# Attention scores of all four sequences behind the second gate product, and other places for turns, routing and picking in the last group

## Chip, cores and metric

The kernel runs on one core of one Trainium2 chip. The metric is device time in microseconds (us), the median of several runs; lower is better. All data is float32.

## What is computed

The input is 64 audio signals of 80000 samples. Each is cut into 157 frames of 512 samples (the last one padded), and each frame gets a discrete cosine transform, which gives a matrix of 157 tokens x 512 channels per signal. One transformer layer follows:

```
h = frames @ D^T                                     # DCT, 157 x 512 per signal
x = layernorm(h)
k, q = tanh(x Wk) pi, tanh(x Wq) pi                  # 4 sets x 8 planes of phases
total = sum over sets, planes of  w_s * Re( cumsum(e^{ik} V) e^{-iq} ),  V = x Wv + bv
pos   = the same with fixed phases of the position
gate  = sigmoid(x Wg + bg)
h = h + x + (gate * total + (1 - gate) * sigmoid(pw) * pos) / sqrt(8 t) @ Wo + bo
x2 = layernorm(h)
idx = argmax(mean over tokens of x2 @ Wg' + bg')     # one of 16 experts per signal
h = h + softmax value of idx * (x2 We[idx] + be[idx])
```

Because the phases are few, the cumulative sums are written as a causal attention: scores are cosines of phase differences, summed over sets and planes, times a mask.

## The kernel before, in words

The 64 signals are worked on in 16 groups of four (`GB = 4`, `NG = 16`). Of the 157 tokens of a signal the first 128 make one full tile; the 29 left over of all four signals, the tails, share a fifth tile (index `GB`). The order of all instructions on every engine is written out by hand, so what stands earlier in the code stands earlier in each engine's queue. For a group g from 1 to 15 one turn of the main loop is:

1. `project_and_values(g)`: phases of group g, the values V, and routing and picking for group g-1. `pick` ends with the row numbers of the chosen experts, `fetch` (L707) starts four gathering DMAs of 1 MB of expert weights each from the POOL queue.
2. `gate(g)` (L871): five small gathering DMAs for the expert biases (`bias`, L744) and two additions of the value bias (`add_bv`, L348, 128x1024 each) go into the POOL queue, together with the subtraction of one frame (`fold_once`, L97). Then the gate is computed by a Strassen-like scheme with seven products in the order 1, 2, 6, 5, 7, 3, 4. `gate_product` (L534) issues eight matmuls into one PSUM tile; `gather` (L288) then adds the tile to the partial sums on VectorE (L286; product 1 is copied by ScalarE, L295). The products share three PSUM tiles in rotation (`ps_mm`, 3 buffers). Product 5 is kept in its tile (`held`) until the second of the two additions that follow product 7; product 4 gets that same tile.
3. Between the products stand the scores: `scores(0)` and `scores(2)` each make two matmuls (L559), one VectorE multiplication of the PSUM result by a mask (L561) and one VectorE addition of two SBUF operands (`att` and `share`, L562, 128x314). `scores_of_tails` makes one matmul (L566), one multiplication (L567) and one addition of two SBUF operands (L570, 128x116). Their PSUM tiles come from the other pool (`ps_tr`, 2 buffers). Before the change `scores(0)` stands behind the first product, `scores(2)` behind the third, `scores_of_tails` behind the fourth.
4. `experts_and_embedding(g)`: the expert products of group g-1 mixed with the transform of group g+1.
5. `attention(g)`: reading values with the scores, and the output product.

Group 0 has a start of its own. After the loop stands the code of the last group (L962 to L998): the expert products of group 14 (`expert(g - 1, ...)`), between which group 15 is normalised (`normal2`, ScalarE, L650), transposed (`turn_x2`: four transposes on TensorE, L166, and a copy out of PSUM), routed (`route`, `route_sum`, `route_spread`) and picked; then four weight fetches, `pick_gate`, five bias gathers, the two expert products of group 14 that are left, and the five of group 15 in the order 0, 1, 2, tails, 3. `expert` calls `between(c)` ahead of the two matmuls of each quarter c of its contraction. The first two fetches go to the rooms of `wv` and `wg`, which are free by then; the other two to the weight buffers that group 14's first two experts leave. The bias `be_last` gets the router's weight and the residual added (`add_bias`, L755) before the expert's PSUM tile is added (L774), and only then is that PSUM tile free.

`place` (L169) writes the copy of a transposed tile. For a full tile it uses the engine that is passed as `copy`; for the tails' tile it used ScalarE always.

Of the kernel before, what the change touches and what calls it, by code (L numbers as in the profile page):

```python
# [22 lines left out]
P = 128  # L23
C = D // P
H = D // 2
GB = 4
# [13 lines left out]
ORDER = [GB, *range(GB)]  # L40
# [3 lines left out]
def audio_tower(ctx: ExitStack, tc: tile.TileContext, a, out):  # L44
# [15 lines left out]
    nc = tc.nc  # L60
# [14 lines left out]
    def psum():  # L75

        return ps_mm.tile([P, 2, 512], F32, tag="mm", name="mm")

    def bank():
        return ps_tr.tile([P, 512], F32, tag="tr", name="tr")  # L80
# [10 lines left out]
    def fold_once(g, m):  # L91

        if g < NG:
            ft = S[g]["frame", m]
            even = p2.tile([P, 2, P], F32, tag="even", name="even")
            nc.vector.tensor_tensor(even, ft[:, :2, :], ft[:, 2:, :], ALU.add)
            nc.gpsimd.tensor_tensor(ft[:, :2, :], ft[:, :2, :], ft[:, 2:, :], ALU.subtract)  # L97
            S[g]["even", m] = even

    def fold_twice(g, m):  # L100

        if g < NG:
            ft, even = S[g]["frame", m], S[g].pop(("even", m))
            nc.vector.tensor_tensor(ft[:, 2, :], even[:, 0, :], even[:, 1, :], ALU.add)
            nc.vector.tensor_tensor(ft[:, 3, :], even[:, 0, :], even[:, 1, :], ALU.subtract)
# [57 lines left out]
    def transposed(x):  # L163
        tr = bank()
        for c in range(C):
            nc.tensor.transpose(tr[:, c * P : (c + 1) * P], x[:, c * P : (c + 1) * P], ident)  # L166
        return tr

    def place(xT, m, tr, apart=None, copy=nc.scalar.copy):  # L169

        if m < GB:
            copy(xT[:, :, m, :P], tr.rearrange("p (c t) -> p c t", c=C))
            return
        nc.scalar.copy(xT[:, :, :, P:], tr.rearrange("p (c b t) -> p c b t", c=C, b=GB))
        if apart is not None:
            nc.scalar.copy(apart, tr.rearrange("p (c t) -> p c t", c=C))

# [4 lines left out]
    def by_tokens(ps, lhs, w):  # L182

        for c in range(C):
            nc.tensor.matmul(ps, lhs(c), w[:, c, :], start=(c == 0), stop=(c == C - 1))  # L185
        return ps
# [159 lines left out]
    def add_bv(g, m):  # L346
        v = S[g]["v2", m]
        nc.gpsimd.tensor_tensor(v, v, bv.unsqueeze(1).to_broadcast([P, 2, D]), ALU.add)  # L348
# [185 lines left out]
    def gate_product(g, i):  # L534

        s = S[g]
        if i == 1:
            s["gT"] = p1.tile([P, C, GB, LP], F32, tag="gT", name="gT")
        ps, rhs, w = psum(), operand(i, s["xT"], s["sums"]), fac_g[i]
        for o in range(2):  # L540
            for c in range(2):
                nc.tensor.matmul(  # L542
                    ps[:, o, : 2 * L], w[:, c, o * P : (o + 1) * P], rhs[:, c], start=(c == 0), stop=(c == 1)
                )
        part = [[s["gT"][:, 2 * n : 2 * n + 2, 2 * m : 2 * m + 2, :L] for n in range(2)] for m in range(2)]
        gather(i, by_halves(ps), part, s)
        for k, m, n in ((2, 0, 0), (7, 1, 1), (3, 0, 1), (4, 1, 0)):
            if k == i:
                for o in range(2):
                    to = part[m][n][:, o]  # L550
                    c = 2 * n + o
                    nc.scalar.activation(to, to, AF.Tanh, bias=hbg[:, c : c + 1], scale=0.5)  # L552

    def scores(i):

        two = slice(i, i + 2)
        ps = bank()[:, : 2 * L].rearrange("p (b t) -> p b t", b=2)
        for b in range(2):
            nc.tensor.matmul(ps[:, b], kf[:, i + b, :P], qf[:, i + b, :L], start=True, stop=True)  # L559
        every = lambda x: x.unsqueeze(1).to_broadcast([P, 2, L])  # L560
        nc.vector.tensor_tensor(att[:, two, 0, :], ps, every(hmask), ALU.mult)  # L561
        nc.vector.tensor_tensor(att[:, two, 1, :], att[:, two, 0, :], every(share), ALU.add)  # L562
# [90 lines left out]
    def turn_x2(g, m, copy=nc.scalar.copy):  # L653
        s = S[g]
        if m == GB:
            s["x2T"] = p1.tile([P, C, GB, LP], F32, tag="xT", name="x2T", bufs=2)
        place(s["x2T"], m, transposed(s.pop(("x2", m))), copy=copy)


    def route(g):  # L660

        s = S[g]
        s["each"] = ps = bank()
        for c in range(C):
            for b in range(GB):
                nc.tensor.matmul(  # L666
                    ps[TL * b : TL * (b + 1), :L], rwg[:, c, :], s["x2T"][:, c, b, :L], start=(c == 0), stop=(c == C - 1)
                )
# [6 lines left out]
    def route_spread(g):  # L675

        s = S[g]
        s["all"] = ps = bank()
        nc.tensor.matmul(ps[:, :P], s.pop("tot").to_broadcast([P, P]), ident, start=True, stop=True)

    t = lambda name, shape, dt=F32: p2.tile(shape, dt, tag=name, name=name)
# [3 lines left out]
    def pick(g):  # L685

        s = S[g]
        lg = s.pop("all")[:, :P].rearrange("p (b e) -> p b e", b=GB)[:, :, :E]
        s["logit"] = logit = t("logit", wide)
        nc.vector.scalar_tensor_tensor(logit, lg, 1.0 / L, rbg, ALU.mult, ALU.add)  # L690
        s["top"] = top = t("top", [P, GB])
        nc.vector.tensor_reduce(top, logit, AX.X, ALU.max)

        score = t("score", wide)
        nc.vector.tensor_tensor(score, logit, over(top), ALU.is_equal)
        nc.vector.tensor_tensor(score, score, revexp, ALU.mult)
        s["rev"] = rev = t("rev", [P, GB])
        nc.vector.tensor_reduce(rev, score, AX.X, ALU.max)
        s["rows"] = rows = t("rows", [P, GB], I32)
        nc.vector.tensor_scalar(rows, rev, float(-P), rowbase, ALU.mult, ALU.add)  # L700
        s["ws"] = []
# [34 lines left out]
    def bias(g, m):  # L736
        s = S[g]
        if g + 1 < NG:
            be = p2.tile([P, D], F32, tag="be", name="be", bufs=NM)
        else:  # L740

            be = p1.tile([P, C, P], F32, tag="frame", name="be_last", bufs=NM).rearrange("p c t -> p (c t)")
        s["be", m] = be
        nc.gpsimd.indirect_dma_start(  # L744
            out=be,
            out_offset=None,
            in_=a["be"],
            in_offset=bass.IndirectOffsetOnAxis(ap=s["expi"][:, m : m + 1], axis=0),
        )
# [7 lines left out]
    def expert(g, m, between=lambda c: None):  # L757
        s = S[g]
        xT, ws = s["x2T"], s["ws"]
        ps = psum()[:, 0, :]  # L760
        if m < GB:
            by_tokens(ps, lambda c: between(c) or xT[:, c, m, :P], ws[m])
        else:
            for c in range(C):
                for i in range(GB):
                    nc.tensor.matmul(  # L766
                        ps[TL * i : TL * (i + 1), :],
                        xT[:, c, i, P:],
                        ws[i][:, c, :],
                        start=(c == 0),  # L770
                        stop=(c == C - 1),
                    )
        o = s.pop(("be", m))
        nc.vector.scalar_tensor_tensor(o, ps, s["gate"][:, m : m + 1], o, ALU.mult, ALU.add)  # L774
        if m < GB:
            nc.sync.dma_start(out=out[GB * g + m, :P, :], in_=o)
        else:

            for i in range(GB):
                for lo, hi in ((0, TL // 2), (TL // 2, LT)):  # L780
                    queue = nc.sync if g + 1 < NG else nc.scalar
                    queue.dma_start(out=out[GB * g + i, P + lo : P + hi, :], in_=o[TL * i + lo : TL * i + hi, :])
# [88 lines left out]
    def gate(g):  # L871
        for m in range(NM):
            bias(g - 1, order[m])
        add_bv(g, 0)
        add_bv(g, 1)
        fold_once(g + 1, 2)
        for n, i in enumerate(PRODUCTS):
            gate_product(g, i)
            if n == 0:
                scores(0)  # L880
            elif n == 2:
                scores(2)
            elif n == 3:
                scores_of_tails()
            elif n == 4:
                fold_twice(g + 1, 2)
# [75 lines left out]
    g = NG - 1  # L962
# [6 lines left out]
    normal2(g, 2)  # L969
    normal2(g, 3)  # L970

    def turns(c):
        if c == 2:
            turn_x2(g, 2)
        elif c == 3:
            turn_x2(g, 3, nc.vector.tensor_copy)

    def routes(c):
        if c == 1:
            route(g)  # L980
            route_sum(g)
        elif c == 3:
            route_spread(g)

    expert(g - 1, ORDER[1], turns)
    expert(g - 1, ORDER[2], routes)
    pick(g)

    fetch(g, range(GB), [w.rearrange("p c o -> p (c o)") for w in (wv, wg)])
    pick_gate(g)  # L990
# [94 lines left out]
```

## Time and profile before

| what | us |
|---|---|
| median of 3 runs | 1482.98 |
| the three runs | 1480.23, 1483.87, 1482.98 |
| the profiled execution | 1479.63 |
| its span (first to last instruction) | 1477.8 |
| TensorE busy | 1449.9 (98%) |
| VectorE busy | 981.5 (66%) |
| GpSimd (POOL) busy | 696.3 (47%) |
| ScalarE busy | 482.9 (33%) |
| one group, first read matmul (L583) to the next (703.72 to 794.41) | 90.7 |

The profile is one execution. Engines: PE is TensorE's matmuls, PEld its weight loads, DVE VectorE, ACT ScalarE, POOL GpSimd, SP the engine that issues most DMAs. A line such as `L562` is a line of the kernel. In the chain of waits each row has a start, a length, and what the end of the kernel hung on in that time. In a timeline a row has start, busy time, engine, line, operation, tiles and, in brackets, idle time before it and what ended it. A wait row reads: who, for whom, us in total, times, longest.

### The profile page before, as it was taken

The page shows a single profiled execution, that of the slowest core. Times are in us where ns is not written, and L with a number is a line of the kernel's source. Part 1 is how long each engine was busy: PE and PEld are TensorE (multiplying, and loading weights), DVE is VectorE, ACT ScalarE, POOL GpSimd, SP SyncE. Part 2 cuts the span into 40 slices and gives each one's busy share as a digit, 9 for nine tenths or more (in the row PEclk, how much of TensorE's full clock was granted, in tenths as well). Part 3 has the DMA queues.
Part 4 walks back from the last instruction along what each step waited for, and adds up shares of the span by engine and source line. Part 5 has one row for each costly group of instructions (what it writes and reads, how often), then busy time and mean ns, then how long its engine had stood idle before and what let it go on. Part 6 is the DMA issues. An engine that isn't in the chain of part 4 may idle for free.

```text
span 1477.8 us, 19242 instructions
## 1 busy us (share of the span) xinstructions
PE 1449.9 (98%) x6866; PEld 1004.8 (68%) x6866; DVE 981.5 (66%) x2026; ACT 482.9 (33%) x782; POOL 696.3 (47%) x1042
## 2 busy tenths in 40 slices
PE   8999999999999999999999999999999999999997
PEld 5776676767767677675766757667576676767763
DVE  5677676666766667666776666757667676666663
ACT  4532143422424323243232433224332143422410
POOL 4455454454444454454454543546435454454422
PEclk9999999999999999999999999999999999999999
DMA  5104132050321404223041330413205132040305
GB/s 193 36 1 185 36 150 71 8 193 22 149 71 41 167 14 157 64 78 136 7 171 49 116 103 3 179 42 147 74 1 185 35 150 71 6 165 14 150 7 213
DMA packets 42862, 135.36 MB, mean 92 GB/s; under 512 B 7872, under 2 KB 8400, under 8 KB 34192
## 3 DMA queue, kind: packets, MB, share of 16 engines
q0 software_dynamic: 15616, 88.09, 15.7%
q1 hardware_dynamic: 26920, 45.81, 9.6%
q8 instruction: 55, 0.90, 0.3%
q10 hardware_dynamic: 232, 0.24, 0.1%
q14 instruction: 39, 0.32, 0.1%
HBM read 113.53 MB, written 20.58 MB: 91 GB/s over the span
## 4 chain that ended last, share of the span: by engine, by line
PE 87%; DVE 9%; DMA 2%; POOL 1%; issue 1%; ACT 0%; SPq 0%; POOLq 0%; DVEq 0%
PE mm L283 26%; PE mm L185 22%; PE mm L583 9%; PE mm L542 9%; PE tr L166 5%; DVE att L562 5%; PE mm L203 4%; PE mm L766 4%; DVE gT L286 2%; PE mm L488 2%; PE mm L201 2%; PE mm L596 2%; PE tr L666 1%; PE mm L524 1%; DMA be_last<-in_be,expi 1%
## 5 line engine op out<-in xcount | busy, mean ns | idle before, releaser
L185 PE MATMUL mm<-we,x2T 128*128 128x512 f32 x496 | 223.4, 593 | 0.0
L157 POOL TENSOR_SCALAR rstd<-mv 128x1 f32<-128x1 f32 x160 | 47.5, 297 | 320.2 <-DVE mv L155 313.6
L185 PEld LDWEIGHTS mm<-we,x2T 128*128 128x128 f32 x496 | 92.5, 190 | 95.6 <-issue 89.2
L583 PE MATMUL mm<-att,v 128*128 128x314 f32 x512 | 138.2, 427 | 2.4 <-DVE of_tails L574 2.4
L774 DVE SCALAR_TENSOR_TENSOR be<-mm,gate,be 128x512 f32<-128x512 f32 x75 | 56.3, 751 | 125.8 <-PE mm L185 86.5
L213 ACT ACTIVATE x<-mm,shift,rstd 128x512 f32<-128x512 f32 x80 | 62.2, 778 | 223.6 <-POOL shift L160 223.6
L583 PEld LDWEIGHTS mm<-att,v 128*128 128x128 f32 x512 | 97.0, 190 | 38.7 <-issue 2.9
L286 DVE TENSOR_TENSOR v<-mm,v 128x512 f32<-128x512 f32 x105 | 72.3, 688 | 75.6 <-PE tr L166 50.3
L552 ACT ACTIVATE gT<-gT,hbg 128x314 f32<-128x314 f32 x120 | 60.3, 551 | 182.2 <-DVE gT L286 180.6
L286 DVE TENSOR_TENSOR gT<-mm,gT 128x628 f32<-128x628 f32 x105 | 85.0, 810 | 44.6 <-PE mm L542 44.1
L158 POOL TENSOR_TENSOR rstd<-rstd,power 128x1 f32<-128x1 f32 x160 | 108.0, 675 | 13.3
L166 PEld LDWEIGHTS tr<-ident,x 128*128 128x128 f32 x576 | 69.4, 141 | 51.8 <-issue 36.3
L611 POOL TENSOR_TENSOR res<-res,u 128x512 f32<-128x512 f32 x48 | 60.2, 1269 | 73.4 <-DVE u L286 73.4
L166 PE MATMUL tr<-ident,x 128*128 128x128 f32 x576 | 88.1, 276 | 1.3 <-ACT x L650 0.9
L153 DVE BATCH_NORM_STATS2 st<-mm 128x6 f32<-128x512 f32 x80 | 55.9, 698 | 50.4 <-PE mm L203 50.4
L707 POOL DMA_INDIRECT we<-in_we,rows x62 | 61.7, 996 | 56.8 <-PE mm L185 40.5
L283 PE MATMUL mm<-t_o,sum 128*128 128x256 f32 x384 | 88.1, 379 | 0.0
L283 PE MATMUL mm<-t_v,sum 128*128 128x256 f32 x360 | 86.7, 384 | 0.0
L604 POOL TENSOR_TENSOR tT_t<-gT,of_tails 128x116 f32<-128x116 f32 x64 | 30.6, 499 | 118.9 <-DVE gT L574 116.7
L283 PEld LDWEIGHTS mm<-t_o,sum 128*128 128x128 f32 x384 | 73.0, 190 | 16.7 <-issue 7.7
L286 DVE TENSOR_TENSOR res<-mm,res 128x512 f32<-128x512 f32 x96 | 64.5, 685 | 29.7 <-PE mm L283 19.0
L203 PE MATMUL mm<-dct_o,frame 128*128 128x256 f32 x320 | 82.3, 380 | 0.0
(188 smaller groups left out, 3054.8 us busy)
## 6 DMA issues: line engine op xcount, KB each, us to landing
frame<-in_frames SPq DMA_DIRECT2D x80, 256.0 KB
out<-be SPq DMA_DIRECT2D x60, 256.0 KB
out<-be SPq DMA_DIRECT2D x60, 32.0 KB
out<-be SPq DMA_DIRECT2D x60, 26.0 KB
be<-in_be,expi POOLq DMA_INDIRECT x75, 8.9
wv<-in_wv SPq DMA_DIRECT2D x1, 1024.0 KB
wg<-in_wg SPq DMA_DIRECT2D x1, 1024.0 KB
wo<-in_wo SPq DMA_DIRECT2D x1, 1024.0 KB
```

The lines of the kernel that those rows point to most:

```text
L158: nc.gpsimd.tensor_tensor(rstd, rstd, power, ALU.pow)
L166: nc.tensor.transpose(tr[:, c * P : (c + 1) * P], x[:, c * P : (c + 1) * P], ident)
L185: nc.tensor.matmul(ps, lhs(c), w[:, c, :], start=(c == 0), stop=(c == C - 1))
L203: nc.tensor.matmul(by_r[:, 1::2, :], ft[:, i, :], dct_o[:, i, :], start=(i == 0), stop=(i == 1))
L213: nc.scalar.activation(x, h, AF.Identity, bias=shift, scale=rstd)
L283: nc.tensor.matmul(ps[:, b, :], lhs[:, c, b, :P], w[:, c, :], start=(c == 0), stop=(c == 1))
L286: add = lambda to, x, y: nc.vector.tensor_tensor(to, x, y, ALU.add)
L542: nc.tensor.matmul(ps[:, o, : 2 * L], w[:, c, o * P : (o + 1) * P], rhs[:, c], start=(c == 0), stop=(c == 1))
L552: nc.scalar.activation(to, to, AF.Tanh, bias=hbg[:, c : c + 1], scale=0.5)
L562: nc.vector.tensor_tensor(att[:, two, 1, :], att[:, two, 0, :], every(share), ALU.add)
L583: nc.tensor.matmul(ps[:, c, : 2 * L], s["v", i][:, cols], att[:, i], start=True, stop=True)
L707: nc.gpsimd.indirect_dma_start(out=w, out_offset=None, in_=a["we"], in_offset=bass.IndirectOffsetOnAxis(ap=s["rows"][:, b : b + 1], axis=0),)
```

## The change

Three edits:

- `place` uses the engine that is passed for the tails' tile too. Only one call passes another engine than ScalarE for that tile, `turn_x2(g, GB, nc.vector.tensor_copy)` of the last group; this copy moves from ScalarE to VectorE.
- In `gate`, for groups 1 to 15, `scores(2)` and `scores_of_tails` both stand behind the second product (n == 1), where they stood behind the third and the fourth.
- In the last group `turn_x2(g, 2)` stands ahead of the expert product of group 14's first sequence and no longer inside it; `turn_x2(g, 3)` stands behind its first quarter; `route` and `route_sum` behind its third quarter; `route_spread` and `pick` behind the first quarter of the next expert product, where `pick` stood behind all of it.

```diff
@@ place
-        nc.scalar.copy(xT[:, :, :, P:], tr.rearrange("p (c b t) -> p c b t", c=C, b=GB))
+        copy(xT[:, :, :, P:], tr.rearrange("p (c b t) -> p c b t", c=C, b=GB))
@@ gate
             gate_product(g, i)
             if n == 0:
                 scores(0)
-            elif n == 2:
+            elif n == 1:
                 scores(2)
-            elif n == 3:
                 scores_of_tails()
             elif n == 4:
                 fold_twice(g + 1, 2)
@@ last group
-    def turns(c):
-        if c == 2:
-            turn_x2(g, 2)
-        elif c == 3:
-            turn_x2(g, 3, nc.vector.tensor_copy)
+    turn_x2(g, 2)
 
     def routes(c):
         if c == 1:
+            turn_x2(g, 3, nc.vector.tensor_copy)
+        elif c == 3:
             route(g)
             route_sum(g)
-        elif c == 3:
+
+    def picks(c):
+        if c == 1:
             route_spread(g)
-
-    expert(g - 1, ORDER[1], turns)
-    expert(g - 1, ORDER[2], routes)
-    pick(g)
+            pick(g)
+
+    expert(g - 1, ORDER[1], routes)
+    expert(g - 1, ORDER[2], picks)
```

## The prediction

> **What bounds the kernel now.** I read the page first. TensorE is busy nearly all the time, so only its idle stretches, and whatever follows its last stretch, can be won.
>
> ```profile
> PE 1449.9 (98%) x6866; PEld 1004.8 (68%) x6866; DVE 981.5 (66%) x2026; ACT 482.9 (33%) x782; POOL 696.3 (47%) x1042
> ```
>
> The list of waits says which of these stretches lie where the change works. The 15 waits are one in each of the groups 1 to 15; the third row is a wait of VectorE in the last group, which TensorE inherits.
>
> ```profile
> PE mm L542 <- DVE gT L286: 12.0, 15, 0.9
> ...
> DVE be_last L755 <- DMA be_last<-in_be,expi: 11.9, 1, 11.9
> ```
>
> Next, the chain of waits through the gate of one middle group (its first product starts at 749.29, its last ends where the expert matmuls start, at 766.48). The chain leaves TensorE for VectorE from 756.34 to 764.26, and the piece that matters is one addition that lasts 4.66.
>
> ```profile
> 752.10 4.24 PE mm L542 x16
> 756.34 0.02 issue
> 756.36 0.81 DVE gT L286
> 757.18 0.40 DVE att L561
> 757.58 0.02 issue
> 757.60 4.66 DVE att L562
> 762.26 0.72 DVE gT L286
> ...
> 764.26 2.38 PE mm L542 x8
> ```
>
> The same L562 of the first pair of scores takes 0.49 at 752.65, so 4.66 is no work. The timeline of POOL shows what covers it: the two value bias additions, started before it and over at 761.86.
>
> ```profile
> 757.19 4.67 POOL L348 TENSOR_TENSOR v<-v,bv 128x1024 f32<-128x1024 f32 x2
> ```
>
> Behind the held L562 VectorE queues the additions of products 6, 5 and 7; the second addition of product 7 frees product 5's PSUM tile, which product 4 needs. Hence TensorE's wait at 764.26.
>
> Last, the chain through the end of the last group: the weight fetches, then the first bias, which lands behind 4 MB of weights; only then do two VectorE steps free the PSUM tile that the tails' expert product waits for.
>
> ```profile
> 1444.43 7.74 PE mm L185 x18
> 1452.17 0.93 POOL we L707
> 1453.09 0.30 issue
> 1453.40 11.38 DMA be_last<-in_be,expi
> ...
> 1466.46 3.64 PE mm L766 x32
> ```
>
> **What the Trainium skill says.** "SBUF — State Buffer", section "Who interferes with whom": VectorE and GpSimd share one pair of SBUF ports; a VectorE instruction with two SBUF inputs contends with a GpSimd instruction that reads SBUF, and the second to start is blocked for the whole of the first, while a VectorE instruction with at most one SBUF input does not contend. The trace agrees on both: L562 (two SBUF inputs) is stretched from 0.49 to 4.66, to just behind POOL's end; and in the attention stage, while POOL adds `bo` (699.95 to 706.1), the VectorE steps L573 and L574 with one PSUM and one SBUF input take 0.49, as they do at 709.64 and 710.15 without POOL. In the list of line L286 none of the 105 gate additions exceeds 0.815. "DMA: Bandwidth & Descriptors", section "Queues, rings and completion order": each DMA engine takes packets of the queues in turn. That bears on the end, where output stores run beside the fetches; the trace shows those DMA engines fully busy (share 0.90 to 1.08 in each stretch from 1450 to 1466).
>
> **The change part by part: the gate.** Nothing is added or removed; two matmuls of `scores(2)`, one of the tails, and four VectorE steps move forward. I lay the products end to end with the lengths of the middle group: a product takes 2.11 (749.29 to 751.40), a pair of scores 0.53, the tails' matmul 0.22.
>
> - TensorE: product 1 to 751.40, scores(0) to 751.93, product 2 to 754.05, scores(2) to 754.58, tails to 754.80, product 6 to 756.91, 5 to 759.03, 7 to 761.14, 3 to 763.26, 4 to 765.37.
> - VectorE: adds product 2 at 754.32 as before, free at 755.05. Scores(2)'s matmul is done by then (its result came 0.2 after its issue ended at scores(0): 751.93 and 752.13). L561 from 755.05 (0.48), L562 from 755.57 (0.49), L567 from 756.06 (0.26), L570 from 756.35 to 756.63. POOL's additions start at 757.19: they stand behind nine DMA issues at 1.25 each from 746.00, which the change does not touch. So both steps with two SBUF inputs lie ahead of POOL, the last with 0.84 to spare at its start. POOL's DMA issues beside them don't hold them: L562 at 752.65 ran in 0.49 beside the issue at 752.46.
> - The additions of products 6 (757.1), 5 (759.2), 7 (761.35 and 762.1) now run while POOL adds. They have one SBUF input each, and I take them at 0.81 (0.73 start to start), not held. Product 7's second addition ends at 762.9; product 4 wants its tile at 763.26. No wait is left, by 0.36.
> - PSUM for the scores: the tails take the tile of scores(0), freed at 752.6, needed at 754.58. `fold_twice` (L104, two SBUF inputs) now comes at 762.9 instead of 764.97; it needs POOL's L97, done at 762.85. A few tenths there move product 3's addition, whose tile isn't needed until the second expert-stage tile at about 768.8: nothing.
>
> The gate ends at 765.37 instead of 766.48: 1.11 less, made up of 1.00 of wait and 0.11 by which the first matmul behind it is longer (532 against 426 ns). For group 1 the wait is 0.45 instead of 0.83, so 0.73; for group 15 it is 0.74, so 1.02. Sum: 13 x 1.10 + 0.73 + 1.02 = **16.05**. Is it given back? The expert weights that follow were issued from 746.0 on; the slowest landing in the list of that line is 11.9, so 757.9 for the first, ahead of 765.4. From there to the next gate TensorE has no wait in the chain, and VectorE's and POOL's work follows TensorE. In group 15 the five bias additions (L755) stand between the last gate addition and the reading of the tails; TensorE's 2.43 wait for these keeps its length and moves forward.
>
> **The last group.** On the clock of the trace before (leaving out the 16.05):
>
> - The tails' copy on VectorE: price unknown for this shape, bounded by ScalarE's 0.59 and VectorE's 0.69 for a full tile; I take 0.69. It waits for the expert addition L774 to 1434.1, so 1434.8, and the second turn needs its PSUM tile: TensorE waits 0.65 (from 1434.15). It takes the copy out of ScalarE's queue, so x of sequence 1 starts at 1432.4 instead of 1434.39 and that wait (up to 1435.26) goes. Then x of sequence 2: ScalarE copies turn 0 until 1434.9 and normalises until 1435.6; the turn of 2, now ahead of the expert, waits 0.4. Together 1.05 instead of 1.11: no gain, no loss. The bound is 0.6 later if ScalarE's order slips by one copy.
> - From 1436.1: expert quarter 0.86, turn 3 0.44, two quarters 1.72, route 1.21, quarter 0.86, next expert's first quarter 0.86, spread 0.22: 1442.27. Pick starts 0.2 later and takes 1.5, as from 1445.99 to 1447.50; rows at 1443.95. First fetch 0.8 later (1447.50 to 1448.28 before): 1444.75 instead of 1448.28, so **3.5 earlier**. It hides one old delay: pick stood behind the L774 of the second expert. The fourth fetch's buffer is left at 1444.96, it issues at 1448.5. The five bias issues follow on POOL, 3.5 earlier too; their row numbers come from `pick_gate` by 1447.
> - The first bias then lands at 1461.25 if DMA moves alike. One more 256 KB store (second expert, 1445.9) falls beside the fetches; at the 400 GB/s of those stretches that is 0.65. I take 0.5 to 0.65: 1461.85. Two VectorE steps (1464.78 to 1466.46, 1.68): the tails start at 1463.5 instead of 1466.46: **3.0 less**. TensorE's own floor, without the 2.19 wait for the first weights, is 1452.1 + 3 x 3.43 = 1462.4, so the gain is 4.0 at most. The lower bound is 2.0 (the stores cost twice what I take and the turns 0.4). Everything behind it is unchanged.
>
> **Sum.** 16.05 + 3.0 = 19.05. The span of 1477.8 becomes 1458.75, the profiled execution's 1479.63 becomes 1460.6. That execution lies 3.35 below the median of the runs; I take the difference off the median: 1482.98 - 19.05 = **1463.9**.
>
> **Rivals.**
>
> 1. *The port catches VectorE after all* (slower). If the tails' addition L570 starts more than 0.84 later than I lay it, behind 757.19, POOL holds it until 761.86; it ends at 762.1 and the additions of 6, 5, 7 and 7 follow at 0.75 each, until 765.1. Product 4 starts at 765.15 against 764.26 now: 0.89 more in each of 15 groups, 13.4, less 3.0 at the end: **1493.4**. The same happens nearly to the letter if PSUM additions were held by POOL. For it: the margin is less than one VectorE step. Against: the order ahead of it is the same every 90.7, and L286, L573 and L574 run unhindered beside POOL. Chance 0.04.
> 2. *L562 is slow for its place among the scores, not for POOL*: then it would still take 4.66, from 755.57; the additions end at 763.8, and the gate wins only 0.4: 15 x 0.4 + 3.0 = 9, **1474**. Against: its end follows POOL's in groups 1, 2, 3 and 15 as well. Also here: part of the gate's gain given back in the expert stage. Chance 0.07.
> 3. *The gates win, the end does not*: the turn ahead of the expert, or DMA contention, eats the 3.5. **1467**. For it: four transfers and stores share full DMA engines. Chance 0.10.
> 4. The forecast, own range 1460 to 1469: 0.79.
>
> About 0.3% (4.4) is what a measurement of this kernel can tell from no change. Cases 2 to 4 are faster by more than that, nearly all; a little of case 2 falls within: faster 0.93, same 0.03, slower 0.04. The range goes from 1459.5 (the end gains 4.0, and runs scatter by 3.6 as the three shown) to 1470 (a quarter of the gate's gain missing and the end's lower bound).
>
> **What would show it.** Right: the wait of L542 on L286 gone from the list of waits; L562 at most 0.5 everywhere; POOL's L348 still 4.67, the gate additions at 0.81 beside it; a group period of 89.6; first fetch 3.5 earlier against the start of group 14's tails expert (1429.64), and the tails' product following its neighbour by about 1. Wrong: a long L570 or L286 beside L348, a new wait between gate and attention, or a bias landing no earlier than before.

## Result and the profile after

| | median us | runs | lowest to highest |
|---|---|---|---|
| before | 1480.57 | 6 | 1479.41 to 1483.87 |
| after | 1501.97 | 6 | 1498.23 to 1505.60 |

The ratio is 1.0139, with a 95% interval of 1.0118 to 1.0159: the change made this run of the kernel slower by 1.4%, where 1463.9 was predicted. The profiled execution took 1499.42, its span is 1497.7. As will be seen, this is not the result on every chip; another chip gave 0.9884.

The engine totals hardly tell it. TensorE's busy time grew by 2.8, VectorE's by 16:

```profile
PE 1452.7 (97%) x6866; PEld 1006.7 (67%) x6866; DVE 997.8 (67%) x2027; ACT 482.5 (32%) x781; POOL 695.5 (46%) x1042
```

The list of waits (who, for whom, us in total, times, longest) does. The wait that was to go has nearly tripled, in 14 of the 15 gates. A wait of the second score multiplication L561 is new, and it too is there 14 times. The bias at the end is waited for 3.2 less:

```profile
PE mm L542 <- DVE gT L286: 32.9, 14, 2.5
...
DVE be_last L755 <- DMA be_last<-in_be,expi: 8.7, 1, 8.7
...
DVE att L561 <- PE tr L566: 7.6, 14, 0.6
```

The chain of waits through the gate of the same middle group (it starts at 762.47 here) leaves TensorE at 769.25, and the held L562 is longer than it was before (each matmul of the code leaves two records, so the pair's two count as x4 and the tails' one as x2):

```profile
765.28 2.11 PE mm L542 x8
767.39 0.53 PE tr L559 x4
767.92 1.33 PE tr L566 x2
769.25 0.47 DVE att L561
769.72 0.03 issue
769.75 5.69 DVE att L562
775.44 0.20 DVE att_t L567
775.64 0.02 issue
775.66 0.49 DVE att_t L570
776.15 0.73 DVE gT L286
776.89 0.04 issue
776.93 4.50 PE mm L542 x16
```

Two rows matter. The tails' matmul seems to last 1.33; it lasts 0.21 in this kernel's own gate of group 15, the one that ran as predicted. And L562 lasts 5.69, though VectorE's timeline has it start 0.63 ahead of POOL's first addition, with 0.49 of work to do. Here is POOL:

```profile
770.38 4.67 POOL L348 TENSOR_TENSOR v<-v,bv 128x1024 f32<-128x1024 f32 x2
```

and VectorE behind it (start, busy time, and in brackets the idle time ahead):

```profile
767.84 0.81 DVE L286 TENSOR_TENSOR gT<-mm,gT 128x628 f32<-128x628 f32 x1 [1.52 <-PE mm L542]
769.23 0.48 DVE L561 TENSOR_TENSOR att<-tr,hmask 128x314 f32<-128x314 f32 x1 [0.57 <-PE tr L566]
...
776.08 3.49 DVE L286 TENSOR_TENSOR gT<-mm,gT 128x628 f32<-128x628 f32 x4
```

L561 was laid directly behind the addition of product 2; it stands idle for 0.57 behind it (TensorE began the pair's scores at 767.23), and 6.76 behind the gate's start instead of 5.76. So L562 falls into POOL's hold, and the four additions of products 6, 5, 7 and 7 stand behind it. Product 3 wants product 6's PSUM tile and waits 2.44.

The last group did what it was to do. The first weight fetch is issued 15.40 behind the start of group 14's tails expert instead of 18.64, and the tails' product starts 61.9 behind the last gate instead of 65.1. The chain of waits of this profile shows neither a fetch nor a bias there; it runs from TensorE's third expert product, which ends at 1485.53, straight to the addition L774 of the first expert. That is a coincidence. The first expert's product was over at 1478.67, and L774 starts 0.86 behind the bias step L755, as it did before (1464.80 and 1465.66). VectorE's timeline has what it waited for:

```profile
1484.67 0.75 DVE L755 SCALAR_TENSOR_TENSOR be_last<-be_last,gate,res 128x512 f32<-128x512 f32 x1 [8.65 <-DMA be_last<-in_be,expi]
1485.53 0.75 DVE L774 SCALAR_TENSOR_TENSOR be_last<-mm,gate,be_last 128x512 f32<-128x512 f32 x1
```

So the first bias still ends the wait. TensorE stands idle for 0.80 ahead of the tails' product at 1486.33, where it stood for 1.58 before.

TensorE's timeline cuts every kernel of this study into four parts, which I use from here on: up to the first gate (group 1), the 15 gates (first product to the first matmul behind product 4), the 14 stretches between gates, and what follows the last gate. The middle gate is that of group 8.

| trace | chip | start | gates | between | end | a middle gate |
|---|---|---|---|---|---|---|
| before | no number | 114.8 | 257.5 | 1029.0 | 76.4 | 17.19 |
| after | no number | 113.9 | 281.5 | 1029.0 | 73.2 | 18.80 |
| after, again (below) | 12 | 114.3 | 242.9 | 1028.9 | 74.7 | 16.10 |

Of the 19.9 by which the span grew, the gates gave 24.0, the end took back 3.2 and the start 0.9. In after 11 of the gates take 18.5 to 18.85 and two take 20.49. In these two, groups 2 and 7, TensorE's granted clock is 0.5 for 3.4 behind the wait, so that products 3 and 4 last 6.35 and 6.39 together instead of 4.66: the gate is 1.7 longer for it. Of the others group 1 takes 18.12, and the gate of group 15 takes 16.10 with L561 at 5.76, as predicted.

### The profile page after: what moved, and what is told of

It is laid out like the page before. It is cut to its first block, busy times and chain, and to the rows that moved or that the text cites. A ratio compares the mean times of both kernels' runs of the same rounds, so it can differ in the third digit from the quotient of the medians.

```text
span 1497.7 us, 19257 instructions
## 1 busy us (share of the span) xinstructions
PE 1452.7 (97%) x6866; PEld 1006.7 (67%) x6866; DVE 997.8 (67%) x2027; ACT 482.5 (32%) x781; POOL 695.5 (46%) x1042
## 4 chain that ended last, share of the span: by engine, by line
PE 90%; DVE 8%; issue 1%; POOL 0%; DMA 0%; ACT 0%; SPq 0%; POOLq 0%; DVEq 0%
PE mm L283 25%; PE mm L185 23%; PE mm L542 9%; PE mm L583 9%; PE tr L166 5%; PE mm L203 4%; DVE att L562 4%; PE mm L766 4%; PE mm L488 2%; PE mm L201 2%; PE mm L596 2%; DVE att_t L570 1%; PE tr L666 1%; PE tr L566 1%; PE tr L559 1%; PE mm L524 1%
## 5 line engine op out<-in xcount | busy, mean ns | idle before, releaser
L774 DVE SCALAR_TENSOR_TENSOR be<-mm,gate,be 128x512 f32<-128x512 f32 x75 | 56.3, 751 | 126.4 <-PE mm L185 87.2
L286 DVE TENSOR_TENSOR v<-mm,v 128x512 f32<-128x512 f32 x105 | 72.3, 688 | 75.6 <-PE tr L166 50.3
L286 DVE TENSOR_TENSOR gT<-mm,gT 128x628 f32<-128x628 f32 x105 | 85.2, 811 | 44.9 <-PE mm L542 37.9
L542 PE MATMUL mm<-sum,wg 128*128 128x314 f32 x240 | 72.3, 446 | 32.9 <-DVE gT L286 32.9
L286 DVE TENSOR_TENSOR res<-mm,res 128x512 f32<-128x512 f32 x96 | 64.4, 685 | 29.7 <-PE mm L283 19.0
```

What stands on the lines that cost most here:

```text
L286: add = lambda to, x, y: nc.vector.tensor_tensor(to, x, y, ALU.add)
L542: nc.tensor.matmul(ps[:, o, : 2 * L], w[:, c, o * P : (o + 1) * P], rhs[:, c], start=(c == 0), stop=(c == 1))
```

## The experiments

Times are medians beside the kernel before on the same chip; a ratio comes with its 95% interval. "Behind the gate" counts from the start of its first product.

**One part at a time, and two other places (chip 6).** The profile names the tails' matmul L566 as what released L561. So the first theory was that this matmul, which takes the PSUM tile of scores(0), drags the wait of the pair with it; the rivals were the place itself, whatever the tile, and an interaction of gate and last group. Four kernels. The last group's edits alone (gate as before):

> Only the edits of the last group and of `place`; the gates stay as before. Both theories (tile wait, crowding) put all the loss into the gates 1 to 14 and let the last group win: 3.2 less than before (73.27 against 76.45 from the first tails reading to the end, in the two traces), so 1477.4 for a median of 1480.6, and the gates' wait of 12.0 in total as before. If the last group's edits took part in the loss, this would be slower than before.

1476.39 against 1480.09, 0.9975 [0.9964, 0.9985]: 3.7 less. The gate edit alone (last group as before):

> Only the edit in the gate; the last group stays as before. Both theories: about 1.7 more in each of the groups 1 to 14, 1.0 less in group 15, so some 23 over before, 1503 to 1505. Should the two parts not add up (the sum of this difference and that of the last group alone not near +20), they would act on each other.

1465.58, **0.9906** [0.9889, 0.9922]. The gate edit, which was expected to lose some 23, won 14.5. In its trace L561 starts 5.76 behind the gate and the gates take 16.10, all but that of group 1. The tails' scores into unused columns of the pair's PSUM tile, so that they wait for nothing:

```diff
-    def scores(i):
+    def scores(i, tails=False):
+        tile = bank()            # the pair in [:, : 2 * L]
...
+        if tails:
+            nc.tensor.matmul(tile[:, 2 * L : 2 * L + GB * LT], kf_t, qf[:, :, P:L], ...)
```

> As changed, but the tails' score matmul writes into unused columns of the PSUM tile of scores(2) and stands ahead of its VectorE steps, so that it no longer waits for scores(0)'s tile to come back; its only wait is for POOL's kf_t, done 10 us before. Order and work on VectorE are the same. Theory 'tile wait' (a matmul that waits in TensorE's queue for VectorE makes TensorE's later signals come late, by 1.3 for scores(2)): L561 starts 5.76 after the gate's start, as in group 15, all steps with two SBUF inputs are over before POOL's additions, gates of 16.1, the 1463.9 of the prediction within 3. Theory 'crowding' (the signals come late because three groups of score matmuls stand behind one product, or because of the DMA landings in that stretch): L561 at 6.8 as in the changed kernel, about 1501.

1463.21, 0.988 [0.9863, 0.9896]. And only scores(2) moved, the tails left behind the fourth product:

```diff
-            elif n == 2:
+            elif n == 1:
                 scores(2)
             elif n == 3:
                 scores_of_tails()
```

> As changed, but the tails' scores stay behind the fourth product as before; only scores(2) moves up behind the second. Theory 'tile wait': no early wait, so L561 at 5.76 and L562 over by 6.8, ahead of POOL (7.90). The tails' addition L570 then falls under POOL until about 13.0, product 7's additions follow and product 4 starts about 0.5 late: gate 16.6, 0.6 less than before, about 1469 with the last group's gain. Theory 'crowding' by three groups of score matmuls: also no late signal here, so the same; by DMA landings: L561 at 6.8, L562 held until 13, about 1500.

1461.38, 0.9871 [0.9854, 0.9887]. Here the tails' addition does fall into POOL's time, and is held, but only for the remaining 2.0:

```profile
752.38 1.99 DVE L570 TENSOR_TENSOR att_t<-att_t,share_t 128x116 f32<-128x116 f32 x1
```

Product 7's additions follow early enough (the expectation had product 4 about 0.5 late), and all 15 gates take 16.10, group 1's too. None of the three in which scores move showed the slowness of after. Either the edits spoil each other in their first form, or the chip matters.

**The changed kernel again, with its parts (chip 12).** Unchanged; the gate edit alone again; the gate edit with the copy of the tails' tile on VectorE; the gate edit with the new order, the copy on ScalarE.

> The changed kernel once more, unchanged. The edits of the last group alone gave 1476.4 and the edit in the gate alone 1465.6, so by addition the changed kernel should take 1461.9. Theory 'interaction': the two parts slow each other although the last group's code stands behind all gates of the program; then 1500 again, with L561 at 6.8 behind the gate's start. Theory 'state of that load': the late signals belonged to one loading or one chip, and this gives about 1462, with L561 at 5.76.

> The gate edit alone once more, unchanged, to see whether 1465.6 comes again. 'Interaction': 1465.6 within 2. 'State of that load': 1465.6 mostly, 1503 if this load falls into it.

> The gate edit and the tails' copy on VectorE, with the order of the last group as before. 'Interaction' through the number of instructions on ScalarE or VectorE (one moves from one to the other): about 1500. 'Interaction' through the last group's order, or 'state of that load': 1465 less the 0.5 of the copy.

> The gate edit and the last group's new order, with the tails' copy on ScalarE as before. 'Interaction' through the last group's order: about 1500. 'Interaction' through the copy, or 'state of that load': 1465.6 less some 3, 1462.5.

| kernel | median us | ratio |
|---|---|---|
| before | 1479.72 | |
| the change, unchanged | 1462.43 | 0.9884 [0.9868, 0.9901] |
| gate edit alone | 1465.31 | 0.9903 [0.9883, 0.9923] |
| gate edit and copy | 1465.53 | 0.9904 [0.9887, 0.9920] |
| gate edit and order | 1462.29 | 0.9885 [0.9869, 0.9902] |

The same kernel that took 1501.97 takes 1462.43 here. There is no interaction: order gives 3, the copy nothing. VectorE's timeline in the same group (gate from 742.92) is the predicted one:

```profile
747.95 0.81 DVE L286 TENSOR_TENSOR gT<-mm,gT 128x628 f32<-128x628 f32 x1 [1.18 <-PE mm L542]
748.68 0.47 DVE L561 TENSOR_TENSOR att<-tr,hmask 128x314 f32<-128x314 f32 x1
749.19 0.48 DVE L562 TENSOR_TENSOR att<-att,share 128x314 f32<-128x314 f32 x1
749.60 0.27 DVE L567 TENSOR_TENSOR att_t<-tr,hmask_t 128x116 f32<-128x116 f32 x1
749.90 0.28 DVE L570 TENSOR_TENSOR att_t<-att_t,share_t 128x116 f32<-128x116 f32 x1
```

with POOL behind it:

```profile
750.81 4.68 POOL L348 TENSOR_TENSOR v<-v,bv 128x1024 f32<-128x1024 f32 x2
```

L561 follows its neighbour without a gap, and nothing is held. TensorE's orders, matmul for matmul, are the same in both traces. What differs is when its signals arrive. A step that needs the result of a matmul waits for a semaphore that TensorE raises; this is called the matmul's signal here. Every signal has its own record; on this chip each comes within 0.07 of the modelled end of its matmul. In after 73 matmuls have none there, and in the gate looked at above the signals come late: the one of scores(2)'s last matmul comes 1.58 behind that matmul's start instead of 0.31, that of the tails' 1.39 instead of 0.29, product 2's 0.79 instead of 0.44. Some records are missing altogether, and a missing record is not by itself a late signal: product 1's has none in its place either, and the ScalarE copy that waits for it starts 2.37 behind the gate on both chips.

**On another chip (15): the change again, and the shared tile beside it.**

> The changed kernel a third time, unchanged. Measured so far: 1502.0 in the first measurement, 1462.4 in the second. Theory 'chip or load': the changed kernel has two times, about 1462 and about 1500, and this falls on one of them, with L561 at 5.76 or at 6.8 behind the gate's start. Theory 'outlier': 1462 from now on.

> The version with the tails' scores in the PSUM tile of scores(2) (no wait of TensorE for scores(0)'s tile), on the same chip as the run before it. If that wait is what can make TensorE's signals late: 1463 also where the changed kernel takes 1500. If the lateness has nothing to do with the wait: slow where that one is slow.

The change: 1500.76 against 1480.67, 1.0138 [1.0096, 1.0181], with L561 6.8 behind the gate, L562 held for 5.6, and again 73 matmuls without a signal in place. The shared tile, which won on chip 6: 1503.87, 1.0159 [1.0124, 1.0195]. So the slowness goes with the chip (or with the visit: no numbered chip was used twice), it comes back at the same size, and the first theory falls: no wait for a PSUM tile is left in this kernel, and it is held all the same.

**Is the lateness there before the change, and does distance cure it (chip 11)?** The kernel before, traced, and a kernel with all scores behind the first product, the tails in the tile of scores(2):

```diff
             if n == 0:
                 scores(0)
-            elif n == 1:
-                scores(2)
-                scores_of_tails()
+                scores(2, tails=True)
```

> The kernel before, unchanged, for a trace on the chip of the run beside it. If this chip is one on which the changed kernel takes 1500: theory 'hidden lateness' says that TensorE's signals are late here as well (the score product L561 of the second pair, or the additions of products 2 and 6, some tenths to 1.3 behind their place), and that the time stays 1480 because L562 is held by POOL until 12.98 behind the gate's start whatever its own start. Theory 'only in the new order' says that all signals are on time here. On another chip: all on time, 1480.

> As changed, but all scores stand behind the first product: scores(0), scores(2) and the tails in the PSUM tile of scores(2). The last step with two SBUF inputs, the tails' addition, starts about 5.0 behind the gate's start instead of 6.98, so 2.2 ahead of the 7.25 from which such steps were held in the traces so far, where the late signals cost 1.0 to 1.1. If the loss comes from late signals that push a step with two SBUF inputs under POOL: 1462 to 1465 on every chip, also where the changed kernel takes 1500. If late signals cost time by themselves: slower than 1470 on such a chip.

Before: 1480.49, 1.0003 [0.9993, 1.0013], all signals in place. This chip has no lateness, so the trace could not answer. All scores behind product 1: **1460.5**, 0.9872 [0.9844, 0.9901]; all gates 16.10.

**The same two once more (chip 14).**

> All scores behind the first product, once more, in the hope of a chip with late signals. There (known by missing or late signals of TensorE between 1 and 10 behind the gate's start): 1460 to 1463 if the loss of the changed kernel comes from steps with two SBUF inputs that start after 7.25; over 1470 if late signals cost time by themselves. On another chip: 1460.5 again.

> The kernel before on the same chip. If signals are late on this chip in the run beside it: 'hidden lateness' expects them late here too, with the time at 1480; 'only in the new order' expects all on time. On another chip: 1480, all on time.

This chip has the lateness: 62 and 51 matmuls have no signal in place. The kernel before shows no loss from it, 1479.95, 1.0 [0.999, 1.001]. Its timeline tells why (gate from 749.30):

```profile
756.37 0.81 DVE L286 TENSOR_TENSOR gT<-mm,gT 128x628 f32<-128x628 f32 x1 [1.23 <-PE mm L542]
758.09 0.48 DVE L561 TENSOR_TENSOR att<-tr,hmask 128x314 f32<-128x314 f32 x1 [0.91 <-PE tr L559]
758.61 3.66 DVE L562 TENSOR_TENSOR att<-att,share 128x314 f32<-128x314 f32 x1
```

L561 waits 0.91 that it does not wait in the profile shown to the prediction, where L562 starts at 757.60. But POOL holds L562 until 762.26 in either. **The late signal was there before, under the cover of POOL's additions**, and the profile of before cannot show it: in its own trace all signals are in place. Whether that trace comes from the chip of the result is not on record.

All scores behind product 1 takes **1461.2** here, 0.9874 [0.9845, 0.9902]. Signals are late in it too: product 2's addition starts 6.78 behind the gate instead of the 5.79 of chip 11, and product 6's 9.56 instead of 7.83. But the two-input steps are long done (gate from 741.27; L579 of this kernel is the tails' addition, L570 elsewhere; "remote" means that the profile names no releaser):

```profile
746.26 0.28 DVE L579 TENSOR_TENSOR att_t<-att_t,share_t 128x116 f32<-128x116 f32 x1
748.05 0.81 DVE L286 TENSOR_TENSOR gT<-mm,gT 128x628 f32<-128x628 f32 x1 [1.51 <-PE mm L542]
750.83 1.73 DVE L286 TENSOR_TENSOR gT<-mm,gT 128x628 f32<-128x628 f32 x2 [1.96 <-remote]
```

**What makes the signals late? Half the weights (chip 10).** In all traces with lateness so far the matmuls whose signals are not in place begin 1.9 to 7.4 behind the gate. In that stretch POOL issues the last of nine gathers, and most of 4 MB of weights arrives. If the bytes do it, half of them should ease it. The gathers fetch 64 of the 128 rows, and the expert products contract over 64: half of that contraction is left out.

```diff
-                out=w,
+                out=w[: P // 2],
-                in_offset=bass.IndirectOffsetOnAxis(ap=s["rows"][:, b : b + 1], axis=0),
+                in_offset=bass.IndirectOffsetOnAxis(ap=s["rows"][: P // 2, b : b + 1], axis=0),
```

> The changed kernel a fourth time, to tell which kind of chip this is: 1462 or 1500.

> As changed, but each weight gather fetches only 64 of the 128 rows, and the expert products contract over these 64 (half of the experts' contraction is left out); TensorE's number of columns and the order of all queues stay. The weight packets then end at about 4 behind the gate's start. On a chip with late signals: theory 'weight traffic' expects none late after about 4.5, L561 at 5.76 in every gate, and about 1461; theory 'something else in that stretch' (bias issues on POOL, the order on TensorE) expects late signals as in the run beside it and about 1498. On a chip without: 1461 and nothing to tell apart.

The change on this chip: 1505.04 against 1479.32, 1.0175 [1.0141, 1.0209]. With half the rows: 1531.63, 1.0355 [1.0325, 1.0385], and L561 later still, 7.5 to 9.6 behind the gate in groups 2 to 14. The expectation from weight bytes failed, in sign. The longer time beside the change is no measure of it: 18.5 of it lie between the gates, and the clock falls to 0.5 in nine gates instead of four, while the others of groups 2 to 14 take 18.7 where they take 18.8 in the change. And the test was not clean: the four gathers hardly became shorter (their packets run for 10.7 instead of 12.1, medians of the 15 gates), the DMA engines were as busy (share 1.01 instead of 0.99 in the first 9 of the gates), and the stretches between the gates grew from 73.5 to 74.8 each.

**The weights behind the biases (chips 9 and 0).** The weight fetches are issued behind the bias gathers, so that the weights' packets run 5.9 to 18 behind the gate instead of −1.5 to 10.5. The order in POOL's queue is all that changes.

```diff
         pick(g - 1)
-        fetch(g - 1, range(GB))
...
             bias(g - 1, order[m])
+        fetch(g - 1, range(GB))
         add_bv(g, 0)
```

> As changed, but POOL issues the five bias gathers ahead of the four weight gathers, so that the weights' packets run from about 5 to 15 behind the gate's start instead of -1.5 to 10.5; POOL's additions start some 1.5 later (9.4). On a chip with late signals: theory 'weight gathers' expects the signals before 5 on time and late ones up to about 14 instead of 8; theory 'that stretch of the gate, whatever is gathered' expects late ones from 2.3 to 8 as before. L561 at 5.76 in the first case. The time tells little here, since POOL starts later: 1460 to 1466 in both unless a late addition delays product 4. On a chip without: all on time.

> The bias gathers ahead of the weight gathers, once more. On a chip with late signals: 'weight gathers' expects late ones from about 7 to 14 behind the gate's start and none before, 'that stretch of the gate' from 2.3 to 8, in both cases 1460 to 1466, since POOL's additions start at 8.93. No late signals again would leave open whether the chip or the order is the reason.

Chip 9 (all signals in place): 1460.45, 0.9869 [0.9841, 0.9898]. Chip 0: 1462.62 against 1478.94, 0.989 [0.9861, 0.9919]. Here 67 matmuls have no signal in place, and they begin 1.9 to 9.5 behind the gate. But the early ones are missing records and no late signals, as far as VectorE's timeline tells, for the steps that wait for them are on time in all 15 gates: product 2's addition at 5.03 behind the gate, L561 at 5.76, L570 at 6.98. What is late is product 6's addition, at 9.1 instead of 7.83, and product 5's, at 10.6 instead of 9.95 (VectorE, gate from 741.51):

```profile
747.27 0.47 DVE L561 TENSOR_TENSOR att<-tr,hmask 128x314 f32<-128x314 f32 x1
...
748.48 0.28 DVE L570 TENSOR_TENSOR att_t<-att_t,share_t 128x116 f32<-128x116 f32 x1
750.63 0.81 DVE L286 TENSOR_TENSOR gT<-mm,gT 128x628 f32<-128x628 f32 x1 [1.87 <-PE mm L542]
```

So neither theory fits in full. With the weights' packets at 5.9 to 18 the early signals are in time, as 'weight gathers' expected; but the late ones end at 10.6 and not at 14. The changed kernel was not run on chip 0, so the order and the chip can't be told apart either.

The kernel is fast here because the pair's signals are in time. POOL's additions also start later, 8.9 behind the gate and not 7.9:

```profile
750.44 4.67 POOL L348 TENSOR_TENSOR v<-v,bv 128x1024 f32<-128x1024 f32 x2
```

With its scores on time the kernel would have been clear of them at 7.9 too. Only in group 1, where POOL was there at 7.6 in the kernels above, does the later start count: its gate takes 16.10 here.

## Why the prediction was wrong, and where it was right

**The step that failed** is the sentence "Scores(2)'s matmul is done by then (its result came 0.2 after its issue ended at scores(0))", and with it "the last with 0.84 to spare at its start". A signal that took 0.2 in one place of one trace was taken for a constant. Of the eight numbered chips four have the lateness (15, 14, 10, 0) and four have not (12, 6, 11, 9); the one of the result, whose number is not known, has it. In the traces of the change that have it the pair's signal comes about 1 later (L561 at 6.76 behind the gate where 5.76 was laid), and that alone passes the margin of L570. For L562, which was laid 1.62 ahead of POOL and is caught in most gates, it takes the next point too.

**The margin itself was smaller than written.** POOL takes the port ahead of its recorded start. Over all traces, 56 steps with two SBUF inputs start 0.01 to 0.65 ahead of the recorded start of POOL's two additions, and all are held; 93 start 0.67 to 0.97 ahead, and none is. It is the start that decides: a step of 0.28 that would have ended 0.34 ahead is held, a step of 0.49 that ends 0.18 ahead is not. The Trainium skill, "Perfetto Trace Analysis", section "GPSIMD Engine Instruction", warns of this: it gives as the recorded start the first read of one of the engine's processors, which comes after the instruction has begun there, and calls the span unreliable. The page gives no size; the boundary found here fits it, at 0.66, but no run shows that this is the reason. So of the 0.91 that the trace on chip 12 shows, 0.25 was to spare. "SBUF — State Buffer", "Who interferes with whom", which the prediction used, is not contradicted: it goes by which instruction is issued first, and the recorded start is not the issue.

**Group 1 shows the margin on a chip without late signals**: its bias gathers start a little earlier against the gate, POOL is there at 7.6, and L570 is caught. From the gate edit alone on chip 6 (gate from 114.04), VectorE, then POOL, then TensorE:

```profile
121.01 5.48 DVE L570 TENSOR_TENSOR att_t<-att_t,share_t 128x116 f32<-128x116 f32 x1
```

```profile
121.63 4.67 POOL L348 TENSOR_TENSOR v<-v,bv 128x1024 f32<-128x1024 f32 x2
```

```profile
127.27 1.06 PE L542 MATMUL mm<-sum,wg 128*128 128x314 f32 x3 [1.20 <-DVE gT L286]
```

The prediction gave this group 0.73 of gain, taking the middle group's order for it. It lost 0.74.

**The gate's sum was right where nothing is late.** On chip 12 the gates of groups 2 to 15 take 15.30 less (predicted 13 x 1.10 + 1.02 = 15.32), 16.10 each where 16.08 to 16.10 was worked out. The stretches between give nothing back: 1029.0 before, 1028.9 after. L286 beside POOL takes 0.81 as in the sum. With group 1 the gates give 14.56 instead of 16.05, and the kernel 17.3 by the medians instead of 19.05. That 1462.43 lies so near to 1463.9 is partly luck: the 1482.98 that the prediction started from is 3.3 above the median of before on that chip.

**The end was right**: 3.2 less in after against a predicted 3.0, by the path that was predicted (the first fetch 3.24 earlier against 3.5, the tails' product 0.80 behind its neighbour against about 1). Over the traces the end takes 73.1 to 76.2 with the new order (13 traces, the one with half the weights not counted, mean 74.5) and 76.1 to 77.8 without (6, mean 76.9). Most of the scatter is the clock: in nine of these 19 traces the granted clock is 0.5 for 3.4 some 5 to 7 behind the last gate. The other ten take 73.1 to 74.1 (6, mean 73.3) with the new order and 76.1 to 76.7 (4, mean 76.5) without. By the medians the order is worth 3.1 beside the gate edit (1465.42 to 1462.36, each the mean of two kernels on chip 12) and 3.7 without it. The copy on VectorE, costed at nothing, is worth nothing.

**Rival 1 is what happened, at a price that was too low.** It let L570 be caught, with 0.89 lost in each gate against before; 1.61 were lost (18.80 against 17.19). The late signal makes L562 the one that is caught, so the tails' two steps come behind the hold too and product 6's addition comes at 776.15, behind the start that product 3 wanted; in the rival only product 4 was late. Where L570 alone is caught, as the rival has it, the gate lost 0.74 (group 1, on the chips without late signals) and 1.3 (groups 4 and 13 of after, in which L562 starts 0.67 ahead of POOL and is let through). Its chance of 0.04 rested on "the order ahead of it is the same every 90.7", which is true of issue and not of signals.

**What stays open.** What delays the signals is not known. Shown: they are late on some chips and not on others, in every kernel traced there, that of before too; nearly all in the one stretch of the gate; and neither the last group's edits nor the PSUM tile is the cause. Not excluded: the weights' gathers. With half the rows, which kept the DMA engines as busy, the signals came later and not earlier; with the weights behind the biases those of the scores came in time, on one chip on which nothing else was traced. Suggested only: the last late signal comes 9.6 to 9.7 behind the gate in most gates of after, where POOL's last gather issue ends at 7.9, and about 1 later when that issue came 1 later. The changed kernel beside the one with the biases first, and a kernel without gathers there, both on a chip with the lateness, would tell; neither was tried. Why chips differ is not known either.

**The best version** is all scores behind the first product: 1460.5 on a chip without lateness, 1461.2 on one with it, 1.3% under before on both, and no slower than the change at its best (1462.43). Biases ahead of weights does about as well (1460.45 and 1462.62). Only scores(2) moved (1461.38) was not run on a chip with lateness; its L562 starts where that of the change does, so the same hold is to be expected there.

## What to carry to other kernels

A margin of a few tenths between engines is none: a step that must not meet GpSimd on the shared ports should be 1 to 2 us clear of it, counted from the record minus 0.66, and in every group, not in the middle one alone. A wait that something else covers says nothing of its own length: before was blind to late signals since POOL held L562 in any case, so moving the step out of the cover bought the lateness with it. And one profile shows one chip; where a change lives on a margin, measure it on several.

## What was not expected of the hardware

- TensorE's signals to VectorE are late by 0.4 to 1.8 in a stretch of the gate on some chips (in the gate looked at 0.35 to 1.27 before POOL's additions, and product 6's 1.82) and within 0.07 of the modelled end on others. It turned one kernel from 0.988 into 1.014 to 1.018 of before, while the medians of the kernel before lay between 1478.9 and 1480.7 on every numbered chip.
- The ports are taken 0.65 to 0.67 ahead of GpSimd's recorded start, and a held step of 128x314 ends about 0.4 behind its recorded end (775.44 and 775.05).
- TensorE's granted clock fell to 0.5 for 3.4 in some of the gates in which product 3 waited for a held addition (2 in after, 4 in the change on chip 10, 4 in the shared tile on chip 15, 9 with half the rows, none in the change on chip 15), and in no gate of the other traces. Each time it cost 1.5 to 1.7.
- Four gathers of 64 rows took 10.7, of 128 rows 12.1: half the rows were nearly as long.
